# A bidirectional selective scan on one core: half groups in order of direction, deeper tiles, softplus and gate on GpSimd, two of four direction sums by accumulating DMA

## The chip, the core and the metric

The kernel runs on one core of a Trainium2 chip. The metric is the device time of one execution in microseconds (us). The core has five engines that each work through an instruction queue of their own: TensorE (PE) for matmuls, VectorE (DVE), ScalarE (ACT), GpSimd (POOL) and SyncE (SP), which here only issues DMAs. DMAs run on 16 DMA engines beside them. In this program a scheduler places instructions into each engine's queue before the run; an engine then takes its queue strictly in order, waiting where an operand or a buffer is not ready.

## The reference, cut to what matters

The network has four layers on x of shape (4, 64, 64, 96). Only layer 0 is touched by the change. It normalizes x in groups of three channels, runs the block below, adds x and applies a relu.

```python
def _L0_conv_ref(x, W_in, conv_w, conv_b, x_proj_w, dt_proj_w, dt_proj_b, A_logs, Ds, W_out):
    xz = x @ W_in.T
    xp, z = (xz[..., :D_INNER], xz[..., D_INNER:])          # 192 channels each
    xc = jax.nn.silu(conv3x3(xp) + conv_b)
    x_hw = xc.reshape(B, D_INNER, L)                         # L = 4096 places, row by row
    x_wh = jnp.transpose(xc, (0, 1, 3, 2)).reshape(B, D_INNER, L)   # column by column
    x_hwwh = jnp.stack([x_hw, x_wh], axis=0)
    xs = jnp.concatenate([x_hwwh, jnp.flip(x_hwwh, axis=3)], axis=0)  # four directions
    x_dbl = jnp.einsum('bdl,cd->bcl', xs, x_proj_w)
    dts, Bs, Cs = ...                                        # 6, 16 and 16 rows
    delta = jax.nn.softplus(dts @ dt_proj_w + dt_proj_b)
    # scan over L:  h = exp(delta * A) * h + (delta * u) * B ;  y = sum_states(h * C)
    y = _selective_scan(xs, delta, A, Bs, Cs, Ds)            # adds D * u
    yy = y[0] + wh_y + inv_y[0] + invwh_y                    # four directions, brought back
    yy = yy * jax.nn.silu(z)
    return yy @ W_out.T
```

The inner dimension has 192 channels with 16 states each, so a batch needs 192 x 16 recurrences of 4096 steps in each of four directions. Layers 1 to 3 (a depthwise convolution, linear attention, a spectral filter and two quantized feed-forward parts) follow, batch by batch.

## The kernel before, in words

`layer0` holds everything that is changed. For each batch it has three kinds of work.

`pre(b)` (L119 to L234) prepares a batch in 8 blocks of 512 places: group norm, the input projection `p_xp` and the gate projection `p_z` (L169, silu L174, stored to `sz_s`), the 3x3 convolution as 36 matmuls (L184) with silu into `u`, `u` stored to `u_s` (L194), the projection to dt, B and C (L198, L202), and the softplus (L212 to L221): |x|, relu and exp and ln on ACT, and five elementwise instructions per 96-channel half on DVE (L216, L219, L220, L221, and L224 for delta times u). delta, delta u, B and C go to DRAM. Five calls of `turn` (L105) then write the transposed (column by column) copies: a load of up to 96 x 4096, and four times an ACT copy (L113) and a store (L117).

The scan stage works on *half groups*: 8 channels x 16 states fill the 128 partitions, and one order of places (o = 0 by rows, o = 1 by columns) is run forward and backward. There are 24 groups x 2 orders x 4 batches = 192 half groups, in the sequence batch, group, order. Each half group has 4 chunks (q) of 1024 places:

- `load` (L267) brings delta (`dl`, 5 buffers) and delta u (`B`, 6 buffers), each 128 x 1024, by SP, broadcast over the 16 states;
- `inputs` (L280, the multiply at L283, POOL) multiplies delta u by the replicated B rows;
- `decay` (L285, L287, ACT) writes exp(delta A) into a PSUM tile `pa` (2 buffers);
- the forward scans (L297, DVE) go over q = 0 to 3 into `S`; then `beside()` is called, which loads the next half group, multiplies its inputs, and takes some steps of work for other batches; then, over q = 3 to 0, come a new `decay`, the reverse scan (L305, DVE, in place in `B`), the sum of both directions (L310, DVE), the multiply by the replicated C rows (L311, POOL), and two matmuls with a matrix of ones that sum the 16 states (L317, four records a chunk in the profile); after each pair of chunks ACT copies the result out (L323) and SP stores it in four pieces (L326).

`replicas(b)` (L331) loads the B and C rows of a batch, for both orders, each 128 x 4096, repeated over 8 channels.

`post(b)` (L236) turns the column-order result back (two `turn` calls into `y2_s`), and then, per block and 96-channel half, loads y, y2, u and silu(z), forms (y + 4 D u + y2) x silu(z) by three DVE instructions (L251, L254, L255), multiplies by W_out (L256) and adds x (L259). All these small tiles and those of `pre` share one ring, `k2`, of 7 buffers of 96 x 512.

`pre(b + 1)` and `post(b - 1)` are generators; the main loop takes their steps inside `beside()`, spread evenly over the 48 half groups of batch b. `pre(0)` runs before the first half group and `post(3)` after the last. Layers 1 to 3 begin after that.

SP's queue holds, in turn, the loads of the next half group, the stores of the last one and the DMAs of the asides. DMAs issued from SP share eight completion slots, so one waits for that issued eight before it.

Of the kernel before, what the change touches and what calls it, by code (L numbers as in the profile page):

```python
# [2 lines left out]

# [1 line left out]

# [5 lines left out]
F32 = mybir.dt.float32  # L11
F16 = mybir.dt.float16
F8 = mybir.dt.float8e5
AF = mybir.ActivationFunctionType
ALU = mybir.AluOpType
# [3 lines left out]
NB = 4  # L19
HW = 64  # L20
L = HW * HW
C = 96
# [29 lines left out]
def layer0(ctx: ExitStack, tc: tile.TileContext, a: dict, x1):  # L52
# [25 lines left out]

    nc.vector.tensor_scalar(d4, d4, 4.0, None, ALU.mult)
    nc.scalar.activation(nega, nega, AF.Exp)  # L80
    nc.vector.tensor_scalar(nega, nega, -1.0, None, ALU.mult)

    def dram(name, shape):
        return [dr.tile(shape, F32, tag=f"{name}{b}", name=f"{name}{b}") for b in range(NB)]
# [4 lines left out]
    bc_s = [dram("bc_s", [2 * NS, L]), dram("bcT_s", [2 * NS, L])]  # L89
    y_s = [dram("y_s", [DI, L]), dram("yT_s", [DI, L])]  # L90
    y2_s = dram("y2_s", [DI, L])
    u_s = dram("u_s", [DI, L])
    sz_s = dram("sz_s", [DI, L])

    def k2(name, shape=(C, BLK)):
        return wk.tile(list(shape), F32, tag="k2", name=name, bufs=7)

    def k10(name):
        return wk.tile([C, RPB + 2, HW], F32, tag="k10", name=name, bufs=2)
# [1 line left out]
    def pre_psum(name, rows=C, cols=BLK):  # L101
        t = ps.tile([128, BLK], F32, tag="pre", name=name, bufs=3)
        return t[:rows, :cols]

    def turn(src, dst):  # L105

        n = src.shape[0]
        t = wk.tile([C, L], F32, tag="turn", name="turn")
        nc.sync.dma_start(t[:n, :], src)
        for q in range(NCH):  # L110
            o = wk.tile([C, CH], F32, tag="turned", name="turned")
            w = CH // HW
            nc.scalar.copy(  # L113
                o[:n, :].rearrange("p (w h) -> p w h", h=HW),
                t[:n, :].rearrange("p (h w) -> p w h", w=HW)[:, q * w : (q + 1) * w, :],
            )
            nc.sync.dma_start(dst[:, q * CH : (q + 1) * CH], o[:n, :])  # L117

    def pre(b):  # L119

# [25 lines left out]
        for i in range(NBLK):  # L146
# [12 lines left out]
            for c in range(2):  # L159
                for ra, rb in ((0, 5), (5, n)):  # L160
# [3 lines left out]
                        start=True, stop=True,  # L164
                    )
                    nc.scalar.copy(xp[:, c, ra:rb, :], p.rearrange("p (r w) -> p r w", w=HW))  # L166
            for c in range(2):
                p = pre_psum("p_z")
                nc.tensor.matmul(  # L169
                    p, lhsT=w_in[:, DI + c * C : DI + (c + 1) * C],  # L170
                    rhs=xb[:, r0 - lo : r0 - lo + RPB, :], start=True, stop=True,
                )
                sz = k2("sz")
                nc.scalar.activation(sz, p, AF.Silu)  # L174
                nc.sync.dma_start(sz_s[b][c * C : (c + 1) * C, cols], sz)
            yield
            u = wk.tile([C, 2, BLK], F32, tag="u", name="u", bufs=2)
            for oc in range(2):
# [12 lines left out]
                    u[:, oc, :], p.rearrange("p r w -> p (r w)"), AF.Silu,  # L191
                    bias=conv_b[:, oc : oc + 1],
                )
            nc.sync.dma_start(u_s[b].rearrange("(c p) l -> p c l", p=C)[:, :, cols], u)  # L194
            yield
            px = pre_psum("p_xd", RK + 2 * NS)
            for c in range(2):
# [6 lines left out]
            for c in range(2):  # L204
                rows = slice(c * C, (c + 1) * C)
                p = pre_psum("p_dt")
                nc.tensor.matmul(p, lhsT=dt_w[:, rows], rhs=xd[:RK, :], start=True, stop=True)


                e = k2("e")  # L210
                r = k2("r")
                nc.scalar.activation(e, p, AF.Abs, bias=dt_b[:, c : c + 1])  # L212
                nc.scalar.activation(r, p, AF.Relu, bias=dt_b[:, c : c + 1])
                nc.scalar.activation(e, e, AF.Exp, scale=-1.0)  # L214
                w = k2("w")
                nc.vector.tensor_scalar(w, e, 1.0, None, ALU.add)  # L216
                lg = k2("lg")
                nc.scalar.activation(lg, w, AF.Ln)
                nc.vector.scalar_tensor_tensor(w, w, -1.0, e, ALU.add, ALU.subtract)  # L219
                nc.vector.tensor_tensor(r, r, lg, ALU.add)  # L220
                nc.vector.tensor_tensor(r, r, w, ALU.subtract)  # L221
                nc.sync.dma_start(delta_s[0][b][rows, cols], r)
                du = k2("du")
                nc.vector.tensor_tensor(du, r, u[:, c, :], ALU.mult)  # L224
                nc.sync.dma_start(du_s[0][b][rows, cols], du)
            yield
        turn(bc_s[0][b], bc_s[1][b])
        yield
        for c in range(2):
# [3 lines left out]
            turn(du_s[0][b][rows, :], du_s[1][b][rows, :])  # L233
            yield  # L234

    def post(b):  # L236

        for c in range(2):
            rows = slice(c * C, (c + 1) * C)
            turn(y_s[1][b][rows, :], y2_s[b][rows, :])  # L240
            yield
        for i in range(NBLK):
            cols = slice(i * BLK, (i + 1) * BLK)
            p = pre_psum("p_out")
            for c in range(2):
                rows = slice(c * C, (c + 1) * C)
                y, y2, u = k2("y_in"), k2("y2_in"), k2("u_in")
                nc.sync.dma_start(y, y_s[0][b][rows, cols])
                nc.sync.dma_start(y2, y2_s[b][rows, cols])
                nc.sync.dma_start(u, u_s[b][rows, cols])  # L250
                nc.vector.scalar_tensor_tensor(y, u, d4[:, c : c + 1], y, ALU.mult, ALU.add)  # L251
                sz = k2("sz_in")
                nc.sync.dma_start(sz, sz_s[b][rows, cols])
                nc.vector.tensor_tensor(y, y, y2, ALU.add)  # L254
                nc.vector.tensor_tensor(y, y, sz, ALU.mult)  # L255
                nc.tensor.matmul(p, lhsT=w_out[:, c, :], rhs=y, start=(c == 0), stop=(c == 1))  # L256
            xr = k2("xr")
            nc.sync.dma_start(xr, a["xT"][:, b * L + i * BLK : b * L + (i + 1) * BLK])
            nc.vector.tensor_tensor(xr, p, xr, ALU.add)  # L259
            nc.scalar.activation(xr, xr, AF.Relu)  # L260
            nc.sync.dma_start(x1[b][:, cols], xr)
            yield

    def chunk(q):
        return slice(q * CH, (q + 1) * CH)

    def load(b, g, o):  # L267

        rows = slice(g * 8, (g + 1) * 8)
        dl, du = [], []  # L270
        for q in range(NCH):
            for dst, src, n, tag, bufs in ((dl, delta_s, "dl", "dl", 5), (du, du_s, "B", "B", 6)):
                t = big.tile([128, CH], F32, tag=tag, name=n, bufs=bufs)
                nc.sync.dma_start(
                    t, src[o][b][rows, chunk(q)].unsqueeze(0).broadcast_to([NS, 8, CH])
                )
                dst.append(t)
        return dl, du

    def inputs(b, g, o, du):  # L280

        for q in range(NCH):
            nc.gpsimd.tensor_tensor(du[q], du[q], reps[o, 0][:, chunk(q)], ALU.mult)  # L283

    def decay(g, dl, q):  # L285
        pa = ps.tile([128, CH], F32, tag="pa", name="pa", bufs=2)
        nc.scalar.activation(pa, dl[q], AF.Exp, scale=nega[:, g : g + 1])  # L287
        return pa

    def scan(b, g, o, dl, B, beside):  # L290

        rows = slice(g * 8, (g + 1) * 8)
        S = []
# [7 lines left out]
        beside()  # L301
        last = None
        for q in reversed(range(NCH)):
            pa = decay(g, dl, q)
            nc.vector.tensor_tensor_scan(  # L305
                B[q][:, ::-1], pa[:, ::-1], B[q][:, ::-1],
                last[:, 0:1] if last is not None else 0.0, ALU.mult, ALU.add,
            )
            last = B[q]
            nc.vector.tensor_tensor(S[q], S[q], B[q], ALU.add)  # L310
            nc.gpsimd.tensor_tensor(S[q], S[q], reps[o, 1][:, chunk(q)], ALU.mult)  # L311

            if q % 2 == 1:
                py = ps.tile([128, BLK], F32, tag="py", name="py")
# [12 lines left out]
                        y_s[o][b][rows, i * BLK : (i + 1) * BLK], ys[32 * j : 32 * j + 8, :]  # L327
                    )

    reps = {}  # L330

    def replicas(b):

        for o in range(2):
            for k in range(2):
                t = big.tile([128, L], F32, tag=f"rep{o}{k}", name=f"rep{o}{k}")
                nc.sync.dma_start(
                    t, bc_s[o][b][k * NS : (k + 1) * NS, :].unsqueeze(1).broadcast_to([NS, 8, L])
                )
                reps[o, k] = t  # L340

    for _ in pre(0):
        pass
    phases = [(b, g, o) for b in range(NB) for g in range(NG) for o in range(2)]
    replicas(0)
    loaded = load(*phases[0])
    inputs(*phases[0], loaded[1])
    for n, (b, g, o) in enumerate(phases):
        here = n % (2 * NG)
        if here == 0:  # L350

            aside = chain(post(b - 1) if b > 0 else (), pre(b + 1) if b + 1 < NB else ())
            n_aside = (NBLK + 2 if b > 0 else 0) + (3 * NBLK + 6 if b + 1 < NB else 0)
            done = 0
        nxt = phases[n + 1] if n + 1 < len(phases) else None
        ahead = []

        def beside():
            nonlocal done
            if nxt is not None:  # L360
                if nxt[0] != b:
                    replicas(nxt[0])
                ahead.append(load(*nxt))
                inputs(*nxt, ahead[0][1])
            while done < min(n_aside, n_aside * (here + 1) // (2 * NG - 6)):
                next(aside)
                done += 1

        scan(b, g, o, *loaded, beside)
        if ahead:  # L370
            loaded = ahead[0]
    for _ in post(NB - 1):
        pass

# [483 lines left out]
```

## Time and profile before

| what | us |
|---|---|
| median of the runs (2: 9248.1 and 9255.0) | 9251.6 |
| the profiled execution | 9232.4 |
| its span, first to last instruction | 9230.6 |
| first forward scan begins | 399.9 |
| last matmul of the scan stage ends | 6803 |
| layers 1 to 3 begin their first convolution | 6949.6 |
| busy in the scan stage: DVE, POOL, ACT, PE | 4821.9, 3819.5, 2683.2, 2533.3 |

The busy time of an engine is the sum of its instructions, not of its waits. In a group of instructions, the columns are the line of the kernel, engine, operation, tile written and read, shape, count; then busy time and the mean of one in ns; then the idle time of the engine just before, and what ended it. Per half group the averages are 2.35 us for a scan chunk on DVE, 1.27 for a sum, 2.65 and 2.37 for POOL's two multiplies and 1.12 for ACT's exponential. The chain that ended last runs through PE in layers 1 to 3 and shows little of the scan stage, so the stage is read from the waits and from the order of time.

### The profile page before, as it was taken

To read this page: it belongs to the slowest core of one execution; us is meant where nothing else is said; L and a number is where in the kernel's file an instruction comes from. 1 tells how busy PE (TensorE), PEld (TensorE's weight loads), DVE (VectorE), ACT (ScalarE), POOL (GpSimd) and SP (SyncE) were. 2 spreads that over 40 slices of the span, in tenths; PEclk is the share of its full clock that TensorE was granted. 3 is DMA by queue.
4 is the path that set the end of the run, shared out by engine and by line. 5 is a ranking of instruction groups with operands and counts; after the bars stand their busy time and mean duration, and the time that the engine had idled before them with its cause. 6 is when DMAs were issued, how large, how long until landed. Compare 5 with 4: busy or idle time off the path is not lost. (4 is left out here: it accounts for less than half of the span.)

```text
span 9230.6 us, 61707 instructions
## 1 busy us (share of the span) xinstructions
PE 4926.6 (53%) x20666; PEld 2210.9 (24%) x20666; DVE 5562.8 (60%) x4102; ACT 3233.3 (35%) x3666; POOL 3839.5 (42%) x1576
## 2 busy tenths in 40 slices
PE   8654554122467512227563122222227988889888
PEld 3211110000112100002110000000004857658576
DVE  1277888576787766777777667888853123231332
ACT  3354544333355543326554333333321021110211
POOL 0056666464566645556665566666630000000000
PEclk9776665555577655558665555555557877687886
DMA  2465665676666667666656676666650000100000
GB/s 61 110 176 145 160 171 145 174 167 168 165 161 151 155 158 174 158 175 153 154 145 157 168 171 155 162 161 156 160 155 19 17 26 1 40 2 17 26 3 26
DMA packets 354042, 1118.17 MB, mean 121 GB/s; under 512 B 54384, under 2 KB 56028, under 8 KB 348380
## 3 DMA queue, kind: packets, MB, share of 16 engines
q1 hardware_dynamic: 353724, 1114.23, 48.6%
q8 instruction: 163, 2.67, 0.1%
q14 instruction: 155, 1.27, 0.1%
HBM read 984.00 MB, written 130.02 MB: 121 GB/s over the span
## 5 line engine op out<-in xcount | busy, mean ns | idle before, releaser
L317 PE MATMUL py<-S,red 128*32 128x512 f32 x3072 | 1331.3, 980 | 3619.3 <-POOL S L311 3614.0
L311 POOL TENSOR_TENSOR S<-S,rep 128x1024 f32<-128x1024 f32 x768 | 1817.8, 2367 | 2090.6 <-DVE S L310 1949.2
L287 ACT ACTIVATE pa<-dl,nega 128x1024 f32<-128x1024 f32 x1536 | 1714.5, 1118 | 2208.4 <-DVE B L305 1053.0
L283 POOL TENSOR_TENSOR B<-B,rep 128x1024 f32<-128x1024 f32 x768 | 2027.1, 2650 | 890.1 <-DMA rep<-bc_s 397.0
L297 DVE TENSOR_TENSOR_SCAN S<-pa,S,B 128x1024 f32<-128x1024 f32 x576 | 1352.9, 2349 | 917.6 <-POOL B L283 731.0
L305 DVE TENSOR_TENSOR_SCAN B<-pa,B 128x1024 f32<-128x1024 f32 x768 | 1787.3, 2327 | 25.8 <-ACT pa L287 8.5
L317 PEld LDWEIGHTS py<-S,red 128*32 128x32 f32 x3072 | 135.3, 134 | 4757.2 <-POOL S L311 4715.8
L184 PE MATMUL p_conv<-xp,conv_w 96*96 96x504 f32 (+3 forms) x2304 | 1055.4, 615 | 1.6 <-ACT xp L166 1.6
L310 DVE TENSOR_TENSOR S<-S,B 128x1024 f32<-128x1024 f32 x768 | 973.7, 1268 | 18.8
L580 POOL MEMSET lt<- 128x4 f32 x32 | 3.3, 105 | 1905.6 <-PE p_gram L583 1755.4
L297 DVE TENSOR_TENSOR_SCAN S<-pa,B 128x1024 f32<-128x1024 f32 x192 | 439.4, 2288 | 536.5 <-POOL B L283 528.3
L323 ACT COPY ys<-py 128x512 f32<-128x512 f32 x384 | 224.4, 584 | 1258.8 <-PE py L317 1253.3
L184 PEld LDWEIGHTS p_conv<-xp,conv_w 96*96 96x96 f32 x2304 | 387.1, 172 | 694.3 <-issue 675.4
L523 PE MATMUL p_l<-x,taps 96*96 96x504 f32 (+3 forms) x576 | 250.2, 598 | 30.0 <-DVE s L500 30.0
L113 ACT COPY turned<-turn 96x1024 f32<-96x1024 f32 (+1 forms) x112 | 217.9, 1945 | 85.6 <-DMA y_s<-turned 25.9
L677 PE MATMUL p_dft<-dft,hb 128*64 128x64 f32 x3072 | 227.4, 318 | 9.4 <-DVE hb L667 9.4
L677 PEld LDWEIGHTS p_dft<-dft,hb 128*64 128x64 f32 x3072 | 225.7, 251 | 11.3 <-DVE hb L667 11.3
L663 PE MATMUL p_h<-w1s,ln_s 97*64 97x64 f32 x3072 | 226.4, 320 | 3.5 <-DVE ln_s L562 3.5
L663 PEld LDWEIGHTS p_h<-w1s,ln_s 97*64 97x64 f32 x3072 | 225.2, 251 | 4.2 <-issue 4.2
L400 DVE COPY o<-p_o 128x192 f32<-128x192 f32 x64 | 22.9, 357 | 313.7 <-ACT o L396 313.7
L216 DVE TENSOR_SCALAR w<-e 96x512 f32<-96x512 f32 x64 | 33.8, 528 | 290.7 <-ACT e L214 289.7
L695 PE MATMUL p_dft2a<-tw,z 128*64 128x128 f32 x1024 | 198.1, 395 | 0.0
(170 smaller groups left out, 5370.2 us busy)
## 6 DMA issues: line engine op xcount, KB each, us to landing
dl<-delta_s SPq DMA_DIRECT2D x384, 512.0 KB
B<-du_s SPq DMA_DIRECT2D x384, 512.0 KB
dl<-deltaT_s SPq DMA_DIRECT2D x384, 512.0 KB
B<-duT_s SPq DMA_DIRECT2D x384, 512.0 KB
y_in<-y_s SPq DMA_DIRECT2D x128, 192.0 KB
rep<-bc_s SPq DMA_DIRECT2D x8, 2048.0 KB
rep<-bcT_s SPq DMA_DIRECT2D x8, 2048.0 KB
tw<-in_dft SPq DMA_DIRECT2D x32, 512.0 KB
```

Of the source, the lines that this page charges most:

```text
L184: nc.tensor.matmul(p[:, ra:rb, ca:cb], lhsT=conv_w[:, kc, ky * 3 + kx, oc * C : (oc + 1) * C], rhs=xp[:, kc, at + ra : at + rb, ca + dx : ...
L283: nc.gpsimd.tensor_tensor(du[q], du[q], reps[o, 0][:, chunk(q)], ALU.mult)
L287: nc.scalar.activation(pa, dl[q], AF.Exp, scale=nega[:, g : g + 1])
L297: nc.vector.tensor_tensor_scan(s, pa, B[q], S[-1][:, CH - 1 : CH] if S else 0.0, ALU.mult, ALU.add)
L305: nc.vector.tensor_tensor_scan(B[q][:, ::-1], pa[:, ::-1], B[q][:, ::-1], last[:, 0:1] if last is not None else 0.0, ALU.mult, ALU.add,)
L310: nc.vector.tensor_tensor(S[q], S[q], B[q], ALU.add)
L311: nc.gpsimd.tensor_tensor(S[q], S[q], reps[o, 1][:, chunk(q)], ALU.mult)
L317: nc.tensor.matmul(py[at : at + 32, :], lhsT=red, rhs=S[q][:, k * BLK : (k + 1) * BLK], start=True, stop=True,)
L323: nc.scalar.copy(ys, py)
L523: nc.tensor.matmul(p3[:, ra:rb, ca:cb], lhsT=taps[:, ky * 3 + kx, :], rhs=x3[:, r0 + dy + ra : r0 + dy + rb, ca + dx : cb + dx], start=(k ...
L663: nc.tensor.matmul(p[half : half + N1, j, :], lhsT=ln3[:, :, n0 + j], rhs=w1s[:, hs], start=True, stop=True,)
L677: nc.tensor.matmul(p[ri * N1 : (ri + 1) * N1, j, :], lhsT=hb[:, :, h0 + j], rhs=dft1[:, ri, :], start=True, stop=True,)
```

## The change

Seven things are altered, all in `layer0`:

1. Half groups run in the sequence batch, order, group: all 24 groups of one order, then all of the other (for the last batch, columns first). `replicas` loads one order's B and C rows, chunk by chunk, with four buffers each, at the last group of a half, and they are handed to the scan as an argument.
2. The turned copies of batch 0 and the turning back of the last batch's column result move beside half groups. `beside_half` writes out by hand which steps of which generator go beside which half.
3. `dl` has 7 buffers, `B` 8 and `k2` 8.
4. The reverse scan of the last chunk takes the `pa` of the forward scan, and computes no new one.
5. The sums of the directions of chunks 3 and 1 are made by a DMA from `B` that accumulates into `S`, issued from POOL's queue. Those of chunks 2 and 0 stay on DVE.
6. Softplus: e + 1 and w - 1 become ACT instructions, and the other three and delta times u go to POOL. Gate: the three instructions go to POOL; 4 D u is now formed in `pre` by ACT and stored in place of u.
7. In `pre`, the gate projection and its silu come after the convolution, next to the other silu, and a table of ACT that holds both exp and ln is loaded by name after it.

```diff
+    def natural_exp():
+        tc.keep_in_program_order(nc.scalar.preload_act_table_set("natural_log_exp_and_others"))
...
-            nc.sync.dma_start(u_s[b].rearrange("(c p) l -> p c l", p=C)[:, :, cols], u)
+            for c in range(2):
+                p = pre_psum("p_z")
+                nc.tensor.matmul(
...
+                nc.scalar.activation(sz, p, AF.Silu)
+                nc.sync.dma_start(sz_s[b][c * C : (c + 1) * C, cols], sz)
+            natural_exp()
+            for c in range(2):
+                ud = k2("ud")
+                nc.scalar.mul(ud, u[:, c, :], d4[:, c : c + 1])
+                nc.sync.dma_start(ud_s[b][c * C : (c + 1) * C, cols], ud)
...
-                nc.vector.tensor_scalar(w, e, 1.0, None, ALU.add)
+                nc.scalar.activation(w, e, AF.Identity, bias=one[:, 0:1])
                 lg = k2("lg")
                 nc.scalar.activation(lg, w, AF.Ln)
-                nc.vector.scalar_tensor_tensor(w, w, -1.0, e, ALU.add, ALU.subtract)
-                nc.vector.tensor_tensor(r, r, lg, ALU.add)
-                nc.vector.tensor_tensor(r, r, w, ALU.subtract)
+                nc.scalar.activation(w, w, AF.Identity, bias=one[:, 1:2])
+                nc.gpsimd.tensor_tensor(w, w, e, ALU.subtract)
+                nc.gpsimd.tensor_tensor(r, r, lg, ALU.add)
+                nc.gpsimd.tensor_tensor(r, r, w, ALU.subtract)
...
-                nc.vector.tensor_tensor(du, r, u[:, c, :], ALU.mult)
+                nc.gpsimd.tensor_tensor(du, r, u[:, c, :], ALU.mult)
...
-                nc.vector.scalar_tensor_tensor(y, u, d4[:, c : c + 1], y, ALU.mult, ALU.add)
+                nc.gpsimd.tensor_tensor(y, y, u, ALU.add)
-                nc.vector.tensor_tensor(y, y, y2, ALU.add)
-                nc.vector.tensor_tensor(y, y, sz, ALU.mult)
+                nc.gpsimd.tensor_tensor(y, y, y2, ALU.add)
+                nc.gpsimd.tensor_tensor(y, y, sz, ALU.mult)
...
-            for dst, src, n, tag, bufs in ((dl, delta_s, "dl", "dl", 5), (du, du_s, "B", "B", 6)):
+            for dst, src, n, tag, bufs in ((dl, delta_s, "dl", "dl", 7), (du, du_s, "B", "B", 8)):
...
         for q in reversed(range(NCH)):
-            pa = decay(g, dl, q)
+            if q < NCH - 1:
+                pa = decay(g, dl, q)
             nc.vector.tensor_tensor_scan(
...
-            nc.vector.tensor_tensor(S[q], S[q], B[q], ALU.add)
-            nc.gpsimd.tensor_tensor(S[q], S[q], reps[o, 1][:, chunk(q)], ALU.mult)
+            if q % 2:
+                nc.gpsimd.dma_start(S[q], B[q], accum_op=ALU.add)
+            else:
+                nc.vector.tensor_tensor(S[q], S[q], B[q], ALU.add)
+            nc.gpsimd.tensor_tensor(S[q], S[q], rep[q], ALU.mult)
...
+    def replicas(b, o):
+        both = []
+        for k in range(2):
+            both.append([])
+            for q in range(NCH):
+                t = big.tile([128, CH], F32, tag=f"rep{k}", name=f"rep{k}", bufs=NCH)
+                nc.sync.dma_start(
+                    t, bc_s[o][b][k * NS : (k + 1) * NS, chunk(q)].unsqueeze(1).broadcast_to([NS, 8, CH])
+                )
+                both[k].append(t)
+        return both
...
+    halves = [(b, o) for b in range(NB) for o in ((0, 1) if b < NB - 1 else (1, 0))]
+    phases = [(b, g, o) for b, o in halves for g in range(NG)]
+    def beside_half(h):
+        b, o = halves[h]
+        first = h % 2 == 0
+        steps = []
+        if h == 0:
+            steps.append((turns(0), 5))
+        if first and b > 0:
+            steps += [(turn_back(b - 1), 2), (post(b - 1), NBLK)]
+        if first and b + 1 < NB:
+            steps.append((before[b + 1], NBLK + 1 if b == 0 else 1))
+        if not first and b + 1 < NB:
+            steps.append((before[b + 1], 2 * NBLK if b == 0 else 3 * NBLK))
+            steps.append((turns(b + 1), 5))
+        if not first and b + 1 == NB:
+            steps.append((turn_back(b), 2))
+        return steps
...
-                if nxt[0] != b:
-                    replicas(nxt[0])
+                ahead.append(replicas(nxt[0], nxt[2]) if g == NG - 1 else rep)
                 ahead.append(load(*nxt))
-                inputs(*nxt, ahead[0][1])
-            while done < min(n_aside, n_aside * (here + 1) // (2 * NG - 6)):
+                inputs(ahead[1][1], ahead[0][0])
+            while done < min(n_aside, -(-n_aside * (g + 1) // (NG - 3))):
```

## The prediction

> **What bounds the kernel now.** I read the page's busy times first, then its costliest groups, the waits, and the order of time in one quiet half group. The profiled execution took 9232.4 us around a span of 9230.6; the median shown is 9251.6, 0.2% more. I sum against the span and add 0.2% at the end.
>
> ```profile
> PE 4926.6 (53%) x20666; PEld 2210.9 (24%) x20666; DVE 5562.8 (60%) x4102; ACT 3233.3 (35%) x3666; POOL 3839.5 (42%) x1576
> ...
> L311 POOL TENSOR_TENSOR S<-S,rep 128x1024 f32<-128x1024 f32 x768 | 1817.8, 2367 | 2090.6 <-DVE S L310 1949.2
> L283 POOL TENSOR_TENSOR B<-B,rep 128x1024 f32<-128x1024 f32 x768 | 2027.1, 2650 | 890.1 <-DMA rep<-bc_s 397.0
> L305 DVE TENSOR_TENSOR_SCAN B<-pa,B 128x1024 f32<-128x1024 f32 x768 | 1787.3, 2327 | 25.8 <-ACT pa L287 8.5
> L310 DVE TENSOR_TENSOR S<-S,B 128x1024 f32<-128x1024 f32 x768 | 973.7, 1268 | 18.8
> ```
> No engine is full. The scan stage (first forward scan at 399.9 us, end 6803.0) is 6403 us, 192 half groups of 33.3; the layers after it take 2281 from 6949.6 and are untouched. DVE needs 4 x 2.35 (L297) + 4 x 2.33 + 4 x 1.27 = 23.8 us per half group.
>
> ```profile
> DVE S L297 <- POOL B L283: 1259.3, 402, 36.4
> SPq L117 <- ACT turned L113: 714.8, 110, 18.1
> ```
> DVE's main wait is for du times B from POOL; SP is long held by the transposing copies.
>
> ```profile
> 5451.79 1.22 DVE L310 TENSOR_TENSOR S<-S,B 128x1024 f32<-128x1024 f32 x1
> 5451.88 3.33 POOL L283 TENSOR_TENSOR B<-B,rep 128x1024 f32<-128x1024 f32 x1
> ...
> 5455.18 2.34 POOL L311 TENSOR_TENSOR S<-S,rep 128x1024 f32<-128x1024 f32 x1
> ...
> 5457.48 3.38 POOL L283 TENSOR_TENSOR B<-B,rep 128x1024 f32<-128x1024 f32 x1
> ...
> 5460.82 2.34 POOL L311 TENSOR_TENSOR S<-S,rep 128x1024 f32<-128x1024 f32 x1
> 5460.89 2.35 DVE L297 TENSOR_TENSOR_SCAN S<-pa,S,B 128x1024 f32<-128x1024 f32 x1 [2.23 <-POOL B L283]
> ```
> A quiet half group takes 28.1 us (first forward scans 5427.2 and 5455.25): POOL's products for the next group alternate with those of this one and leave DVE two gaps of 2.2. Twice POOL's product takes 3.3 instead of 2.34: beside a DVE sum with two SBUF inputs. 192 x 28.1 = 5395, so about 1010 of the 6403 are not quiet: 64 at the start (81.2 for the first half group), 96 at three changes of batch, about 850 beside pre, turns and post (turns 14 each, post blocks 11, steps of pre 3.4).
>
> ```profile
> 5430.50:5438.50 8.00, 2.85 (x8) 0.19 (x4) 3.52 (x3) 1.51 (x3) 8.00 (x4) 0.50 0.01 3
> 5440.00:5456.00 16.00, 3.84 (x8) 0.37 (x8) 15.79 (x9) 6.67 (x7) 8.77 (x4) 0.50 1.00 254
> ```
> The windows view, DMA share and GB/s last: the loads of a half group come as one burst at full share, 4 MB in some 17 to 19 us (2.4 per 512 KB), and then nothing.
>
> **Part 1, two sums by DMA.** Removed: 384 of 768 L310, 487 us of DVE. Unless DVE binds, that is worth nothing by itself: DVE's sum falls to 21.3, below a period already longer. Added: two accumulating DMAs, D3 and D1, in POOL's own queue. In the built order POOL has D3, C2, C3, D1, C0, C1, then the next group's B0 to B3 (in about half of the half groups B0 stands before C0); C is the multiply by C's replicas, R and F the reverse and forward scans, numbers are chunks. C3 waits for D3 to land, and D1 and all that follows queue behind it; C1 waits for D1, and B0 to B3, which start DVE's next scans, queue behind that.
> No row has such a DMA. Landing: a lone 384 KB store of a turned tile keeps ACT 3.2 to 3.6 us from its issue; a second load behind a 512 KB one took 6.4 (issued 406.12, used 412.55), so 6.4 - 2 x 2.4 = 1.7 is fixed. A plain 512 KB copy is then 1.7 + 2.0 = 3.7; reading S as well as B makes three streams of two, 1.7 + 3.0 = 4.7, my value for D1. D3 starts in the tail of the loads' burst: 5.7. Low end 3.7 each, high end 1.7 + 4 x 2.4 = 11.3 (twice the bytes at half the share). Issue on POOL: 0.5 (SP's issue of such a load) to 2.3 (a POOL product); I take 1.0.
> Chain from the start of R3: R3 ends 2.3, R2 4.7, its sum 5.9, R1 8.25, R0 10.6, sum 11.8. D3 issued by 3.4, landed 9.1; C2 5.9 to 8.3; C3 to 11.4; D1 issued by 12.4, landed 17.1; C1 to 19.5. Then B0 to B3 (4 x 2.34) and F3 (2.35) to 31.2. With B0 before C0, C1 also ends at 19.5; F1 then needs matmul 1.92, ys 0.58, pa 1.12 (ACT's order puts this ys ahead) and gaps, 3.8, and three scans of 2.36: 30.4. Mean 30.8, against 28.1: 192 x 30.8 = 5914, a loss of 519 from the quiet work. In general the period is 20.4 plus both landings (here 10.4) while the landings bind; the floor with instant landings and issue 0.6 is 29.0.
> The Trainium skill, "DMA: Bandwidth & Descriptors", section "Anatomy of one DMA — SWDGE (gpsimd) path", gives 2.0 us plus bytes over 436 GB/s for a DMA from GpSimd, 3.2 us for 512 KB, issue included; no run here shows it. By that the period would be near its floor of 29.0 and the total some 350 us lower.
>
> **Part 2, deeper tiles.** dl 5 to 7, B 6 to 8. Loads no longer wait for this group's scans: eight B hold two groups, and only the fourth dl waits, for a pa. In the quiet period this gains nothing more (the loads end about 8 us before B0). Its worth is beside the asides, where SP was held (714.8 us behind turned copies) and B came late.
> **Part 3, softplus and gate.** DVE loses about 230 + 184 us, POOL gains 256 + 192 products of half a tile, about 1.2 each (half of 2.34; bounds 0.7, DVE's row, and 2.34): 538, some 400 in the stage. Three gate products lie before D3 and two before C2, where POOL idles 4 and 2.5 us in the chain above; softplus stands in places before D3 or D1, about 1 us per step exposed. If those covers were gone, all 400 would come in.
> POOL waits on DVE's two-input sums now (2650 mean against 2342 for L283, 237 us). The skill's "SBUF — State Buffer", "Summary: rules for kernel authors", says such pairs block each other fully. So half the sums would save half of it, 118, if POOL were always busy; by the chain POOL waits there for a landing anyway, and I count nothing.
> **ACT and PE.** The reverse scan reuses the last pa: 192 x 1.12 = 215 off ACT; table loads go from 298 to 121 in the built program, 227 off; 256 extra activations of 0.63 are 161. ACT is 42% busy in the stage: nothing. The z matmuls (2 x 0.94) move behind the convolution.
> **Asides, what is left of 850.** 28 turns now lie in the stage (those of batch 0 and of the last batch move in, their four copies each in ACT's queue and five DMAs in SP's, ahead of later loads); each adds 3 MB, 13 us of DMA, to 18 of loads and 4 of sums, 35 against 31: 4 each, 112. Post blocks 1.5 x 24 = 36 (ends 0 and 11). Steps of pre 75 x 1 (ends 0 and 3.4). About 220; bounds 0 and 850.
> **Ends.** Replicas come by chunk, so three forward scans of group 0 run during pre(0); pre's block loses about 3 of 44.6 us (two table loads): first scan equivalent at 365 (355 to 400) instead of 400, and the 64 go. Each of seven changes of half waits for C1 before the last replica and the loads: about 10, 70 together against 96. The tail loses two turns but its gates are slower: 133 instead of 146.6.
> Sum: 365 + 5914 + 70 + 220 + 133 + 2281 = 8983, with 0.2% 9000, 2.7% below the median.
>
> **Rivals.** *A DMA wait takes the sums' place (slower).* The landings decide. Break-even is a period of (9231 - 365 - 70 - 220 - 133 - 2281) / 192 = 32.1, both landings 11.7, only 1.3 above mine; 2% slower at 12.7. For it: C3, C1, D1 and B share one in-order queue, and D3 meets the burst. Against: the bus is empty 8 us or more per half group. At 13.5 the period is 33.9, total 9577 + 0.2% = 9600. Chance 0.30.
> *The asides keep half their price (within 2%).* 425 instead of 220: 9188, 9205 with 0.2%. For it: PE's convolutions and the turned copies still hold ACT and SP. Chance 0.20.
> *Landings hidden (faster still).* The floor: 192 x 29.0 = 5568, 8637, 8655. Chance 0.12.
> *DVE was the bound.* All 840 us off DVE would come back: 8390. Against: its gaps end at POOL. Chance 0.03.
> My forecast has 0.35. About 2% is what a measurement can tell from no change: faster 0.50, same 0.20, slower 0.30. The range takes in the floor and most of the slow case: 8640 to 9620.
>
> **What would show it.** Right: a quiet half group of 30 to 32 us, POOL's L334 waiting for the DMA of S, DVE waiting 9 us for L302, DVE near 4000 us in the stage; B no longer waiting for its load. Wrong: a period above 32.1, or asides of 400 and more. The landing of D3 and D1 decides most.

## The result and the profile after

| kernel | median us | runs | ratio to before, 95% interval |
|---|---|---|---|
| before | 9251.55 | 2 (9248.08 to 9255.01) | |
| after | 10288.88 | 2 (10276.8 to 10300.97) | 1.1121 [1.1062, 1.1180] |

The change makes the kernel 11% slower: 1037 us more. The forecast was 9000. The profiled execution spans 10274.9 us.

From the page of after: busy times, the costliest groups and the accumulating DMA's row (the last number there is the median time from the start of the issue to the landing):

```profile
PE 4351.4 (42%) x20666; PEld 2172.8 (21%) x20666; DVE 4825.9 (47%) x3208; ACT 2899.5 (28%) x3489; POOL 4504.9 (44%) x2408
...
L334 POOL TENSOR_TENSOR S<-S,rep 128x1024 f32<-128x1024 f32 x768 | 1831.0, 2403 | 1420.8 <-DMA S<-B 1041.7
L302 POOL TENSOR_TENSOR B<-B,rep 128x1024 f32<-128x1024 f32 x768 | 1833.8, 2434 | 790.9 <-DMA B<-duT_s 409.5
...
L316 DVE TENSOR_TENSOR_SCAN S<-pa,B 128x1024 f32<-128x1024 f32 x192 | 439.5, 2289 | 1882.2 <-POOL B L302 1796.0
...
L331 POOL DMA_DIRECT2D S<-B x384 | 334.5, 871 | 881.5 <-DVE B L325 783.0
L333 DVE TENSOR_TENSOR S<-S,B 128x1024 f32<-128x1024 f32 x384 | 569.7, 1484 | 12.6
...
S<-B POOLq DMA_DIRECT2D x384, 512.0 KB, 5.7
```
DVE lost 737 us of work (5562.8 to 4825.9) and the kernel became slower: its idle time grew by more. In the waits (total, times, longest) DVE's wait for du times B went from 1259.3 to 3265.6, and POOL has a wait that was not there, for the DMA that it issued itself:

```profile
DVE S L316 <- POOL B L302: 3265.6, 462, 106.6
...
POOL S L334 <- DMA S<-B: 1041.7, 258, 10.3
```

A quiet half group, one in the last batch with nothing beside it, takes 33.8 us instead of 28.1. In order of time (start, duration, engine, line, operation; idle time before and what ended it):

```profile
7556.35 0.52 SPq L293 DMA_DIRECT2D dl<-delta_s  x1
...
7561.36 0.55 SPq L293 DMA_DIRECT2D B<-du_s  x1
7562.02 4.74 DVE L325 TENSOR_TENSOR_SCAN B<-pa,B 128x1024 f32<-128x1024 f32 x2
...
7564.89 0.88 POOL L331 DMA_DIRECT2D S<-B  x1 [5.67 <-DVE B L325]
...
7568.11 2.33 POOL L334 TENSOR_TENSOR S<-S,rep 128x1024 f32<-128x1024 f32 x1 [2.35 <-DVE S L333]
...
7576.08 2.34 POOL L334 TENSOR_TENSOR S<-S,rep 128x1024 f32<-128x1024 f32 x1 [5.64 <-DMA S<-B]
7578.36 0.87 POOL L331 DMA_DIRECT2D S<-B  x1
...
7578.97 2.65 POOL L302 TENSOR_TENSOR B<-B,rep 128x1024 f32<-128x1024 f32 x1
...
7581.65 2.29 DVE L316 TENSOR_TENSOR_SCAN S<-pa,B 128x1024 f32<-128x1024 f32 x1 [7.67 <-POOL B L302]
```
Read it downwards. The eight loads of the next half group are issued from 7556.35 to 7561.9. Three microseconds later POOL issues the accumulate of chunk 3 (7564.89), does the product of chunk 2, and then stands for 5.64 us until chunk 3 has landed. Only then come the product of chunk 3, the issue of chunk 1 and du times B, for which DVE has been waiting 7.67 us. The windows of the same stretch (after the engines: granted clock, DMA share, GB/s) show where the accumulate was:

```profile
7556.00:7571.00 15.00, 0.00 (x0) 0.00 (x0) 14.47 (x8) 5.18 (x6) 6.43 (x4) 0.50 0.90 217
7571.00:7576.00 5.00, 0.00 (x0) 0.00 (x0) 2.95 (x2) 0.44 (x1) 0.00 (x0) 0.50 1.04 269
```
The DMA engines are full with the loads until the end; the accumulate's first packet begins at 7571.09, 5.3 us after its issue ended. From the end of its issue chunk 3 lands after 10.1 us (median over the last 900 us of the scan stage), chunk 1, whose DMA finds empty engines, after 3.7. The packets tell where the difference lies: chunk 3's first one begins 5.3 us after the issue and chunk 1's 0.6; from the first to the last they then take 4.1 and 2.8 us.

Read from the first scans of all half groups, the span comes apart as follows. "Above quiet" is what half groups 2 to 191 take over 190 quiet ones; the last part is the last half group, the tail and the layers.

| us | before | after | forecast |
|---|---|---|---|
| second half group starts | 481.1 | 406.4 | 365 + 30.8 = 395.8 |
| 190 quiet half groups | 190 x 28.08 = 5335 | 190 x 33.84 = 6430 | 190 x 30.8 = 5852 |
| above quiet | 955 | 983 | 220 + 70 = 290 |
| from the last half group on | 2459 | 2456 | 30.8 + 133 + 2281 = 2445 |

The forecast lost 578 us in the quiet half group, 693 in what lies beside and 22 at the two ends.

### The profile page after: what moved, and what is told of

It is laid out like the page before. It is cut to its first block, busy times and chain, and to the rows that moved or that the text cites. A ratio compares the mean times of both kernels' runs of the same rounds, so it can differ in the third digit from the quotient of the medians.

```text
span 10274.9 us, 62192 instructions
## 1 busy us (share of the span) xinstructions
PE 4351.4 (42%) x20666; PEld 2172.8 (21%) x20666; DVE 4825.9 (47%) x3208; ACT 2899.5 (28%) x3489; POOL 4504.9 (44%) x2408
## 5 line engine op out<-in xcount | busy, mean ns | idle before, releaser
L340 PE MATMUL py<-S,red 128*32 128x512 f32 x3072 | 747.2, 1015 | 4780.5 <-POOL S L334 4772.9
L334 POOL TENSOR_TENSOR S<-S,rep 128x1024 f32<-128x1024 f32 x768 | 1831.0, 2403 | 1420.8 <-DMA S<-B 1041.7
L302 POOL TENSOR_TENSOR B<-B,rep 128x1024 f32<-128x1024 f32 x768 | 1833.8, 2434 | 790.9 <-DMA B<-duT_s 409.5
L306 ACT ACTIVATE pa<-dl,nega 128x1024 f32<-128x1024 f32 x1344 | 1500.6, 1118 | 2351.3 <-DVE B L325 1140.5
L340 PEld LDWEIGHTS py<-S,red 128*32 128x32 f32 x3072 | 79.8, 137 | 5398.4 <-POOL S L334 5342.0
L331 POOL DMA_DIRECT2D S<-B x384 | 334.5, 871 | 881.5 <-DVE B L325 783.0
L333 DVE TENSOR_TENSOR S<-S,B 128x1024 f32<-128x1024 f32 x384 | 569.7, 1484 | 12.6
L275 PE MATMUL p_out<-y_in,w_out 96*96 96x512 f32 x128 | 129.2, 1113 | 455.4 <-POOL y_in L274 455.4
L233 POOL TENSOR_TENSOR r<-r,lg 96x512 f32<-96x512 f32 x64 | 87.8, 1372 | 293.1 <-ACT lg L230 260.1
```

What stands on the lines that cost most here:

```text
L302: nc.gpsimd.tensor_tensor(du[q], du[q], rep[q], ALU.mult)
L331: nc.gpsimd.dma_start(S[q], B[q], accum_op=ALU.add)
L334: nc.gpsimd.tensor_tensor(S[q], S[q], rep[q], ALU.mult)
L340: nc.tensor.matmul(py[at : at + 32, :], lhsT=red, rhs=S[q][:, k * BLK : (k + 1) * BLK], start=True, stop=True,)
```

## The experiments

Every kernel ran beside the kernel before on the same chip (9240 to 9261 us); a difference to before is taken to that time. Runs without an interval are single ones. "Beside post" are the half groups of the last batch with a step of post, by their first scans.

**Accumulates undone, all and one at a time.** no_acc forms all four sums on VectorE:

```diff
-            if q % 2:
+            if q < 0:
                 nc.gpsimd.dma_start(S[q], B[q], accum_op=ALU.add)
```


> The changed kernel with all four sums of directions on DVE again; all else as changed. Theory 1 (the accumulating DMAs, waited for in POOL's queue, lengthen each half group from 28.1 to 33.8 us): quiet half groups fall back to 28 us, the time to about 10289 - 192 x 5.7 = 9195 us. Rival (softplus and gate on POOL and what they hold up in SP's queue carry the loss): the quiet half group falls but the time stays above 9800 us.

9330.09 us, 90 more than before; quiet 28.0. So the accumulates cost 959 us of the 1037 and all of the quiet loss; but beside post half groups still alternate between 28 and 40.

> Only chunk 1's sum is an accumulating DMA, chunk 3's is on DVE. Theory 1 in its sharper form (the DMA of chunk 3 is issued into the burst of loads and lands 10 us later, that of chunk 1 is issued when the bus is free and lands after 3.7): the quiet half group is about 28.7 us by the chain (chunk 1's landing hides behind the product of chunk 0), the time about 9300. Rival (each DMA costs alike, by its place in POOL's order): about 31 us and 9740.

acc_chunk1 (`if q == 1:`) took 9801.39 us. The quiet half group, 29.2, came near the expected 28.7, but chunk 1 landed after 6.3 us and not after 3.7, and the total missed by 500, since half groups beside work rose to 45. By the total the rival's 9740 was nearer.

> Only chunk 3's sum is an accumulating DMA, chunk 1's is on DVE. Theory 1 in its sharper form: the landing stays near 10 us and everything on POOL queues behind it, quiet half group 33 to 35 us, the time 10200 to 10500, no better than with both. Rival (each DMA costs alike): about 31 us and 9740.

acc_chunk3 (`if q == 3:`) took 9938.82 us: quiet 33.0, landing 10.1. The quiet price is chunk 3's. The total is 350 below after and below the range: half of that comes from quiet half groups (33.0 instead of 33.8), half from what lies above quiet (813 us instead of 983; beside post they are at 40 and not at 45).

> The kernel before with nothing changed but the sums of chunks 3 and 1, which become accumulating DMAs. Theory 1: quiet half groups grow from 28.1 by at least 5.7 us, the time to 10350 or more, since B has only 6 buffers here and is freed only after the landing. Rival (the DMAs cost only in the new order of half groups and with the deeper tiles, whose loads come earlier): under 9700.

before_acc, the kernel before with the accumulates alone, took 10420.53 us, 1180 more than before, with landings of 6.2 and 8.6 us. The rest of the change is not needed for the loss.

**What makes the landing long.** acc_four takes the depth away, so that loads of the next half group cannot be in the air while chunk 3 is summed:

```diff
-            for dst, src, n, tag, bufs in ((dl, delta_s, "dl", "dl", 7), (du, du_s, "B", "B", 8)):
+            for dst, src, n, tag, bufs in ((dl, delta_s, "dl", "dl", 4), (du, du_s, "B", "B", 4)):
```


> The changed kernel with four tiles of delta and four of delta u instead of seven and eight, so that the loads of the next half group cannot be issued while this one's tiles are in use. Theory A (the accumulate of chunk 3 lands after 10.1 us instead of 3.7 because its packets wait behind the burst of 8 loads): with no loads in the air the landing of chunk 3 falls to 3.5 to 5 us after its issue, although the time rises above 11000 us because nothing is loaded ahead. Rival B (the accumulate of chunk 3 is slow for another reason, such as GpSimd's or VectorE's work beside it): it stays at 8 us or more.

Chunk 3 now lands after 3.7 us, with VectorE's scan and sum beside it as in after. The time was not above 11000 but 10189.03, 100 below after, since chunk 1 takes its place: issued among the loads, it lands after 9.0. In order of time:

```profile
7454.76 0.87 POOL L331 DMA_DIRECT2D S<-B  x1
...
7456.07 0.51 SPq L293 DMA_DIRECT2D B<-du_s  x1
...
7466.44 2.34 POOL L334 TENSOR_TENSOR S<-S,rep 128x1024 f32<-128x1024 f32 x1 [5.68 <-DMA S<-B]
...
7481.35 0.88 POOL L331 DMA_DIRECT2D S<-B  x1 [5.66 <-DVE B L325]
...
7484.57 4.64 POOL L334 TENSOR_TENSOR S<-S,rep 128x1024 f32<-128x1024 f32 x2 [2.35 <-DVE S L333]
```
The wait for the DMA has moved from chunk 3 to chunk 1 (5.68 us); at 7484.57 two products run through, chunk 3's without a wait. Whichever accumulate meets the loads pays. It also shows that the deeper tiles brought this kernel nothing.

**Whether POOL's order makes it a loss.** acc_late puts the product of each odd chunk behind that of the even chunk after it:

```diff
-            nc.gpsimd.tensor_tensor(S[q], S[q], rep[q], ALU.mult)
...
+            if q % 2:
+                continue
...
+            for p in (q, q + 1):
+                nc.gpsimd.tensor_tensor(S[p], S[p], rep[p], ALU.mult)
...
```


> The changed kernel (odd chunks summed by DMA), with GpSimd's product of each odd chunk, and its matmuls, moved behind the product of the even chunk that follows it. Theory A (GpSimd, in order, stands idle for the landing, and this is what makes the quiet half group 33.8 us instead of 28): the landing of chunk 3 (10.1 us after its issue) now has VectorE's scan and sum of chunk 2 and one product beside it, that of chunk 1 a product: the quiet half group falls to 28 to 30 us and the time by 4 to 6 us x 192, to 9150 to 9550 us. Rival B (the landing is stretched by whatever the queue carries, and only moves the wait): quiet 33 us or more, 10100 us or more.

10269.59 us, quiet 33.8: theory A's numbers failed. In the built order chunk 1's issue still stood behind chunk 3's product, so the same wait held the same queue. acc_late_loads_act, with the loads from ScalarE's queue too, did no better:

> The same, and the eight loads issued from ScalarE's queue, as in no_acc_loads_act (eight tiles of delta). If both theories A hold (GpSimd idle for the landing in the quiet half groups; SyncE's order beside the asides), the quiet half group is bound by VectorE's eight scans and two sums, 23.4 us, or GpSimd's eight products and two issues, 21.3 us, and lies at 24 to 27 us; beside asides at most 32; time 7900 to 8500 us, less than either kernel. If only the first holds: 9150 to 9550; if only the second: quiet 33 or more, 9200 or more.

10225.51 us, quiet 36.5. ScalarE was now held by loads that waited for a B tile which an accumulate was still reading, and the decays queued behind them: VectorE waited 1972.8 us for pa.

acc_pinned fixes GpSimd's order, with both issues ahead of both waiting products:

```diff
             if q % 2:
-                nc.gpsimd.dma_start(S[q], B[q], accum_op=ALU.add)
+                tc.keep_in_program_order(nc.gpsimd.dma_start(S[q], B[q], accum_op=ALU.add))
             else:
                 nc.vector.tensor_tensor(S[q], S[q], B[q], ALU.add)
...
+                tc.keep_in_program_order(
+                    nc.gpsimd.tensor_tensor(S[q], S[q], rep[q], ALU.mult)
+                )
+        for q in (2, 0):
...
+            tc.keep_in_program_order(
+                nc.gpsimd.tensor_tensor(S[q + 1], S[q + 1], rep[q + 1], ALU.mult)
+            )
...
```


> The changed kernel with GpSimd's order in the reverse half fixed by hand: issue of chunk 3's accumulate, product of chunk 2, issue of chunk 1's accumulate, product of chunk 0, and only then the products of chunks 3 and 1 (in acc_late chunk 1's issue still stood behind the product of chunk 3, so the 10 us landing was only moved). Theory A (GpSimd's in-order wait for the landing makes the 5.8 us between 28.0 and 33.8): both landings lie beside other work, quiet half group 25 to 30 us, time 9300 to 9750 us. Rival B (the DMA itself, its memory traffic beside VectorE and the loads, slows the half group): quiet 33 us or more, 10100 us or more.

9781.32 us, 508 less than after, and quiet 29.2. One such half group:

```profile
7089.96 0.87 POOL L331 DMA_DIRECT2D S<-B  x1
7090.57 2.73 POOL L335 TENSOR_TENSOR S<-S,rep 128x1024 f32<-128x1024 f32 x1
...
7093.25 0.87 POOL L331 DMA_DIRECT2D S<-B  x1
...
7093.86 2.64 POOL L335 TENSOR_TENSOR S<-S,rep 128x1024 f32<-128x1024 f32 x1
...
7096.96 2.34 POOL L340 TENSOR_TENSOR S<-S,rep 128x1024 f32<-128x1024 f32 x1 [0.46 <-DMA S<-B]
7099.26 2.35 POOL L302 TENSOR_TENSOR B<-B,rep 128x1024 f32<-128x1024 f32 x1
...
7103.49 2.34 POOL L340 TENSOR_TENSOR S<-S,rep 128x1024 f32<-128x1024 f32 x1 [1.89 <-DMA S<-B]
```
The waits shrink to 0.46 and 1.89 us because products stand between issue and use. The total slightly missed its range, with some 1340 us above quiet. S tiles are now held longer, until the matmuls have read them: VectorE's wait for that was 121.5 us in after, and is now

```profile
DVE S L316 <- PE py L345: 2281.9, 342, 43.3
```
The quiet half group is no shorter than with VectorE's own sums (28.0): hiding the landings takes most of its loss away and leaves no gain. In the half group above VectorE waits 2.13 and 3.66 us for S tiles, of which there are six; whether more of them would leave a gain was not tried.

**What the rest of the change is worth.** no_acc_gate gives the three gate operations back to VectorE; order_only gives back GpSimd's part of the softplus and the shallow tiles of delta and B too (two steps of the softplus stay on ScalarE).

> no_acc with the three gate operations of post back on VectorE. Theory A (SyncE's order): the k2 tiles are freed by VectorE instead of GpSimd, but SyncE still holds at the same places, so beside post 28/40 us becomes about 28/39, as in the kernel before, and the time is 9250 to 9330 us. Rival B (the gate on GpSimd, 6 products of 1.2 us = 7.2 us in line with the products of the scans, makes the 12 us): beside post about 28/33 us, 54 post steps x 6 = 320 us less, time about 9000 us.

9263.42 us, 10 above before, so GpSimd's gate cost some 80. Beside post 25/41: its place is not what makes the long half groups. (The 54 steps of post in the expectation are 24, so its rival would have given some 150 us and not 320; the pattern beside post decides against it all the same.)

> The order of the half groups, the folded u x D and the split of pre and turns alone: no accumulates, softplus and gate on VectorE, five and six tiles. Theory A (the new order of the half groups is worth about nothing, since a step beside costs the same 10 to 12 us wherever it stands): 9200 to 9330 us. Rival B (the order is worth the 200 to 300 us that it was forecast to give, and the work moved to GpSimd ate them): 8950 to 9100 us.

> order_only once more, in rounds, for an interval: 0.995 of the kernel before, 9200 to 9230 us.

9211.16 us, and in repeated runs 9197.0, ratio 0.9938 [0.9924, 0.9953]. The order of the half groups with the smaller edits is a gain, of 0.6%; softplus on GpSimd and deeper tiles together lose it again (not told apart).

**What the work beside costs, and why.** The loads of the next half group leave SyncE's queue (and delta has eight tiles):

```diff
-                nc.sync.dma_start(
+                nc.scalar.dma_start(
                     t, src[o][b][rows, chunk(q)].unsqueeze(0).broadcast_to([NS, 8, CH])
```


> All four sums on VectorE as in no_acc, and the eight loads of the next half group issued from ScalarE's queue instead of SyncE's, with eight tiles of delta instead of seven so that ScalarE never waits for one that it must free itself. Theory A (a step of pre or post costs 12 us because SyncE, in order, holds at the step's own loads and stores and the next half group's loads stand behind them): the half groups beside post fall from 28/40 us in turn to 28 to 31, the 192 half groups (6478 us in no_acc, of which 5376 are 192 x 28.0) lose at least half of the 1100 us above that floor, and the time is 8500 to 8800 us. Rival B (the step costs what its GpSimd and ScalarE instructions take in line, wherever the loads are issued): beside post still 28/40, time 9250 to 9400 us.

9191.03 us, 62 below before. Beside most steps of post the half groups fell from 28/40 to about 28.5 (32 to 38 beside the first two) and the changes of half from 16 us above quiet to none, as theory A has it. Beside pre they rose to 35 and more, so the total missed both ranges: ScalarE's decays stood behind its loads, and VectorE waited 631.0 and 494.5 us for pa. Three more of this kind follow:

> No accumulates, the gate on VectorE, and the loads of the next half group issued from ScalarE's queue straight behind the four forward decays (pinned there; in no_acc_loads_act they drifted between the decays and held VectorE's scans up). Theory A (SyncE's order makes half of what the asides cost, and the drift of the loads took it back beside pre): about 67 us from the gate as in no_acc_gate, 140 from the loads as in no_acc_loads_act, and 50 to 150 more from the fixed place: 8950 to 9130 us. Rival B (ScalarE, which issues eight loads of 0.6 us, is the new bound beside pre): 9150 to 9300 us.

With the loads pinned behind the forward decays: 9783.61 us, far outside both. The reverse scans waited for pa (949.8 us), which stood behind eight issues that did not go out at once (four in 2.5 us, the fifth 3.3 us after the fourth).

> No accumulates, the gate on VectorE, the loads of the next half group from ScalarE's queue and not pinned (no_acc_loads_act with the gate moved). Theory A (two separate costs: GpSimd's gate 67 us, SyncE's order 140 us): 9080 to 9150 us, 1 to 2% below the kernel before. Rival B (one cost seen twice: the gate on GpSimd waits for loads that SyncE held back, so that with the loads elsewhere the gate's place is indifferent): 9180 to 9230 us.

9096.21 us, ratio 0.9829 [0.9815, 0.9844]: theory A, two separate costs.

> The same with the softplus on VectorE too, as in the kernel before. Theory A (order_only was 52 us below no_acc_gate with the softplus on VectorE and the shallow tiles, so the softplus on GpSimd costs about 50 us): 9030 to 9100 us. Rival B (beside pre ScalarE's queue of loads decides, whichever engine forms the softplus): within 30 us of gate_loads_free.

9007.52 us, 0.9730 [0.9708, 0.9752]: GpSimd's four steps of the softplus back on VectorE gain another 89, more than expected.

Then the stores instead of the loads. Among SyncE's longest waits of no_acc_gate are:

```profile
SPq L349 <- ACT ys L346: 1416.2, 179, 15.6
SPq L120 <- ACT turned L116: 736.7, 111, 18.0
...
SPq L277 <- DVE y_in L270: 300.4, 24, 13.1
```
gate_stores_act moves two stores to the queue of the engine that makes what they store:

```diff
-            nc.sync.dma_start(x1[b][:, cols], xr)
+            nc.scalar.dma_start(x1[b][:, cols], xr)
...
-                    nc.sync.dma_start(
+                    nc.scalar.dma_start(
                         y_s[o][b][rows, i * BLK : (i + 1) * BLK], ys[32 * j : 32 * j + 8, :]
```


> no_acc_gate with the stores of y and of x1, instead of the loads, issued from ScalarE's queue; seven tiles of delta. Theory A (SyncE is held at stores that wait for ScalarE, which would cost ScalarE nothing on its own queue; L349 waits 1408 us and L280 338 us in no_acc): beside post 28/40 becomes 28/32 and the time is 9050 to 9200 us. Rival B (SyncE is held at the loads of post, L277, which still wait for tiles, and not at the stores): beside post still 25/40, 9230 to 9300 us.

> gate_stores_act once more, in rounds, for an interval: ratio to the kernel before 0.915 to 0.920, 8470 to 8520 us.

8489.32 us, and in repeated runs 8479.58, ratio 0.9170 [0.9151, 0.9189], far more than expected: 774 below no_acc_gate. SyncE's longest waits in the stage are now for tiles to come free, each load going out as its tile does:

```profile
SPq L293 <- DVE B L325: 1178.0, 380, 6.7
SPq L293 <- ACT pa L306: 1014.9, 461, 10.4
SPq L120 <- ACT turned L116: 538.8, 98, 15.9
```
All of SyncE's waits for an earlier DMA, those for one of its eight completion slots among them, add up to 1030 us in no_acc_gate and 830 here, so slots can be only a small part of the gain. DVE's wait for du times B is 452.0 instead of 1772.8 in no_acc_gate:

```profile
DVE S L316 <- POOL B L302: 452.0, 27, 104.5
```
A quiet half group takes 27.1 us, half groups beside post mostly 24 to 33, and 484 us lie above quiet instead of 1060. ScalarE does not get the stores for nothing: VectorE's waits for pa rose from 79.3 us to 557.9. The stores of y and of x1 were not tried apart, nor these stores in the kernel before.

Last, the changed kernel with these two stores moved and nothing else:

> The changed kernel with nothing altered but the queue of the stores of y and of x1 (ScalarE's instead of SyncE's). Theory A (two separate costs: SyncE's stores hold the loads, 770 us between no_acc_gate and gate_stores_act; the accumulates' landings hold GpSimd, 959 us between the changed kernel and no_acc): the first goes, the second stays, 9350 to 9700 us. Rival B (the landing was 10 us only because of the burst of loads behind the stores; with the loads spread as tiles come free it falls to 4 to 5 us and the accumulates cost no more than they save): 8400 to 8800 us, landing of chunk 3 under 6 us.

9464.91 us, ratio 1.0228 [1.0202, 1.0254], 985 above the kernel with VectorE's sums and gate. Moving the stores took 824 us off the changed kernel, and the accumulates with the gate cost 985 beside moved stores against 1025 (10288.88 less 9263.42) beside unmoved ones: the two causes are separate. Chunk 3 lands after 5.1 us here and chunk 1 after 6.1, quiet 31.1: without the burst neither is long, and their sum still is. The chain ends elsewhere than in after: it runs from the second landing through GpSimd's products, the matmuls and ScalarE's copy of ys to a pa, for which VectorE waits 1329.6 us (874.2 for du times B), a path that the forecast had for half groups with B0 before C0. SyncE's longest wait in the stage is now for B tiles that an accumulate still reads, 1537.7 us.

## Why the prediction was wrong

**The landing of D3 was mis-sized; the chain was right.** The chain's rule, 20.4 plus both landings, gives 20.4 + 10.1 + 3.7 = 34.2 with the measured landings (33.8 measured), 20.4 + 3.7 + 9.0 = 33.1 in acc_four (33.2) and 20.4 + 5.1 + 6.1 = 31.6 in changed_stores_act (31.1). D1 took 3.7 instead of 4.7, issue 0.87 instead of 1.0 (the fixed part, 6.4 - 2 x 2.4, is 1.6 and not 1.7, which changes little). But "D3 starts in the tail of the loads' burst: 5.7" was wrong: POOL issues it 3.5 us after the last of eight loads, whose packets run until 7577.8, and it lands after 10.1. The burst's 17 to 19 us stood in the forecast's own windows; counted from the issue of its loads, it covers D3. The sum, 13.8 instead of 10.4, is 3.0 us per half group once the chain is followed, 578 us in 190. The slower rival named this mechanism and its price, 13.5 and 33.9, and got 0.30, though the forecast's own windows spoke for it; its 13.5 was a value past break-even and not worked out, so that it fits so well is in part luck. The Trainium skill, "DMA: Bandwidth & Descriptors", section "Anatomy of one DMA — SWDGE (gpsimd) path", gives 2.0 us plus bytes over 436 GB/s for a DMA from GpSimd, an estimate of 3.2 us for these 512 KB with the issue; measured were 0.87 + 3.7 = 4.6 on empty engines and 11.0 in the burst, so the measurement decides.

**The asides kept their whole price, the larger miss.** "Its worth is beside the asides, where SP was held" expected deeper tiles to free the loads: 220 us instead of 850. Measured are 882, and 101 instead of 70 at seven changes of half. SyncE's waits, before and then after, at the loads (L274, L293) and at the stores of ys and xr:

```profile
SPq L326 <- ACT ys L323: 1179.6, 235, 15.1
SPq L274 <- DVE B L305: 816.9, 259, 7.7
SPq L274 <- ACT pa L287: 416.5, 336, 7.4
...
SPq L261 <- ACT xr L260: 175.8, 30, 7.2
```
```profile
SPq L349 <- ACT ys L346: 1688.2, 168, 22.7
...
SPq L280 <- ACT xr L279: 368.8, 31, 15.0
...
SPq L293 <- ACT pa L306: 150.6, 49, 18.7
```
The deeper tiles did what they should: the loads' wait for tiles that an engine held went from 1233.4 us to some 150 (145.7 more for B tiles that an accumulate held). But the queue then stood longer at stores that wait for ScalarE, and POOL's wait for loads of B rose from 493.0 us to 788.3. Two stores on another queue took 774 us off without accumulates and 824 off the changed kernel; four tiles instead of seven and eight made no loss. The forecast had the row of the turned copies (714.8 us) and answered it with more tiles; the larger row for ys it did not have. What makes up the rest, 484 us above quiet without accumulates and some 710 with them after the stores have moved, was not taken apart. That half of the price might stay was a rival with 0.20; that the whole of it and the slow landings come together was in no case, and so none came near 10289.

**Softplus and gate: not settled.** The forecast put them into POOL's gaps beside landings. Without landings the gate cost some 80, and the softplus 89 where the loads ran from another queue. Whether the landings of the changed kernel cover them no run shows.

**Right:** the layers untouched, the start 11 us off, the tail with the last half group 11. The signs named in advance came half true: POOL's L334 waits for the DMA of S, DVE for L302 (7.7 us, 9 forecast), DVE is busy 4128 us from 406 us to 7820 us; but B still waits for its load (L302, 409.5), and the period passed 32.1.

## What to carry over

The sums moved to a DMA were paid here by the engine that used them next, in its queue: count the landing at the place in the DMA traffic where the transfer is issued, and put work of the same in-order queue between issue and use before counting anything as gained. Read what an in-order DMA queue holds: a store that waits for its producer holds every load behind it, and more tiles do not help those loads. Moving two such stores to their producer's queue was worth 774 us here, more than any other edit of the kernel without accumulates. And when two doubtful steps lie on one path, one case of the forecast has to hold both going wrong.

## What was not expected of the hardware

An accumulating DMA of 512 KB issued from GpSimd holds GpSimd 0.87 us and lands 3.7 us later on empty DMA engines, but 9 to 10 us later behind a burst of loads from another queue. Most of the difference lies before its first packet, which began 5.3 us after the issue (3.4 in acc_four) instead of 0.6. Loads issued from ScalarE's queue are not free for ScalarE: with eight in a row its decays came late and VectorE's reverse scans waited 949.8 us for them. Eight short stores per half group there raised all its waits for pa from 79.3 to 557.9 us, less than the 1320.8 us that its wait for du times B lost.
